# Beginning layer 2's first block beside the last pieces of layer 1's expert network

## The chip, the cores and the metric

The kernel runs on one core of a Trainium2 chip. The number that counts is the device time of one execution in microseconds (us). A core has a matrix engine (PE, with its weight loads shown apart as PEld), a vector engine (DVE), an activation engine (ACT), a general engine (POOL) and queues that start transfers (SP's among them). Each works through its own list of instructions in order; between engines, semaphores say when data is ready.

## The reference, cut to what matters

Four layers run over x of 16 sequences x 256 tokens x 128 features. Each layer has an attention part and a feed-forward part, each behind a normalization, scaled and shifted by modulations. The change touches the end of layer 1 and the beginning of layer 2:

```python
# layer 1, feed-forward part: an encoder layer with 8 experts, 2 chosen for each token
gates = softmax(xf @ gW + gb); top2_scores, top2_idx = top_k(gates, 2)
h = relu(einsum('nd,edf->enf', xf, W1) + b1); y = einsum('enf,efd->end', h, W2) + b2
out = einsum('ne,end->nd', w, y)          # w: the two scores, zero elsewhere
# ... then a layer norm, and x = x + gb * out

# layer 2, attention part: 16 heads of 8 features, causal, with rotary positions
h = layernorm(x) * (1 + ca) + sa
Q, K, V = h @ qw, h @ kw, h @ vw          # by heads of 8
Q, K = rope(Q, freq), rope(K, freq)
score = Q @ K.T / sqrt(128) - 1e10 * (1 - tril)
x = x + ga * (softmax(score) @ V) @ ow
```

## The kernel before, in words

x stays in on-chip memory, turned: 128 features on the partitions and 4096 tokens along them, in 8 blocks of 512 tokens (two sequences each).

**Layer 1's experts** (`layer1_ffn`, `sparse`). The tokens of each half of the batch are sorted into lists by expert. The lists are worked off in pieces of 256 rows that belong to one expert, 23 pieces for each half, 46 in all. A step n of the loop in `sparse` fetches the rows and the weights of piece n + 2 (SP), transposes piece n on PE (`ps_in`) and copies it with DVE (`l_x`), does the first product of piece n - 1 (`hidden`: `ps_hid`, then ReLU on ACT into `s`) and the second product of piece n - 2 (`ps_out`, copied by ACT to `l_o` and stored to `done`). At the end of each step, `advance` is called three times.

**Side work as generators.** `self.later` is a list of generators; `advance` gives each of them one step, up to its next `yield`. `tail(blk)` is such a generator. It gathers, by eight indirect transfers that POOL issues, the two expert rows of each token of a block out of `done`, weights and adds them on DVE (`list_sums`), transposes the sum, normalizes it and adds it into x on POOL; then `self.tailed` goes up by one. Tails of the first half are begun at n = 24 (`NPIECE + 1`), when the first half's pieces are stored. Inside the pieces each gather takes two steps, and nine empty steps come after the gathers.

**Layer 2's attention** (`layer2_attn`, `attend8`). A unit is one sequence. For each unit there are two passes over the scores. The first finds the row maxima: eight steps, each with a causal mask (`ident16` times `half_below`), products of `km` with `q` in two groups of 32 partitions into a tile of 1024 columns, and one DVE reduction (L1382). The second pass makes the exponentials of transposed scores with the maxima subtracted (`qm`, `ps_exp`, ACT at L1387, then on POOL at L1390 the part above the diagonal is zeroed) and multiplies them with the values. The loop over `cycle` does one step of the first pass and one of the second, the first pass ahead by `lead = per + LEAD` = 10 cycles. So cycles -10 to -3 are eight cycles of the first unit's maxima alone.

Ahead of a block's first unit, `prepare` must have run: it waits until the block's tail is done (`self.tailed`), normalizes the block (`modulated_steps`, two products with a matrix of means), projects it and rotates it (`turned8`: for each of four tiles, two products on PE, two multiplications on DVE at L1724 or L1722, one addition on POOL at L1725). Then `start_unit` makes `km` on POOL (L1258). At the end of each cycle `advance` is called once and the next block's `prepare` gets one step.

**Order.** With `self.strict` set, PE's instructions stay in the order in which the program makes them. Those of DVE, ACT, POOL and SP are placed by a planner of the framework, which may put an independent instruction earlier. Most operations of these engines go through the helper at L230, products through L273 and transposes through L276, so tiles' names tell them apart.

Of the kernel before, what the change touches and what calls it, by code (L numbers as in the profile page):

```python
# [9 lines left out]
F32 = mybir.dt.float32  # L10
# [4 lines left out]
ALU = mybir.AluOpType  # L15
AX = mybir.AxisListType
# [3 lines left out]
P = 128  # L20
B, T = 16, 256
NT = B * T
BLK = 512
# [192 lines left out]
def bc(ap, shape):  # L216
    return ap.to_broadcast(shape)


class _InOrder:  # L220


    def __init__(self, kernel, engine):
        self.kernel, self.engine = kernel, engine

    def __getattr__(self, name):
        f = getattr(self.engine, name)

        def run(*args, **kw):
            ins = f(*args, **kw)  # L230
# [4 lines left out]
        return run  # L235


class _Kernel:
# [931 lines left out]
    def spaces8(self, pool, nt, ctx):  # L1170


        nc = self.nc
# [3 lines left out]
        self.ps_one = self.pool("ps_two", 2, PSUM, ctx=ctx)  # L1177
        self.v8, self.m8 = [], []
# [32 lines left out]
    def attend8(self, nt, group, prepare, finish, scale, causal=False, masks=(None, None)):  # L1211

        nc = self.nc
        half = self.c("half")
        NQ = nt * P
        qmask, kmask = masks
# [8 lines left out]
            then = [((0, 1), 0, j0) for j0 in (0, 2)]  # L1227
        per = len(first)
        units = group * NBLK
        U = self.units8 = []  # L1230
        sides = []
        ready = {}
        held = []
# [12 lines left out]
        def prepared(blk):  # L1246
            return prepare(blk, lambda: cycle >= (blk - 1) * group * per)

        def start_unit(u):
            blk, i = divmod(u, group)  # L1250
            if i == 0:
                run(ready.pop(blk))
                if blk + 1 < NBLK:
                    ready[blk + 1] = prepared(blk + 1)
            d = U[u]
            km = d["km"] = self.att.tile([P, 2, 2, NQ], F32, tag="km", name="km")
            for i in range(2):
                nc.gpsimd.tensor_scalar(km[:, :, i, :], d["k"], half[:, i : i + 1], 0.0, ALU.mult, ALU.add)  # L1258

# [72 lines left out]
        self.strict = True  # L1332
        lead = per + self.LEAD
        cycle = -lead
        ready[0] = prepared(0)
        for cycle in range(-lead, units * per):
            mx, ex = cycle + lead, cycle
            mu, mt = divmod(mx, per)
            eu, et = divmod(ex, per)
# [53 lines left out]
            held = []  # L1393
# [25 lines left out]
    def layer1_ffn(self):  # L1419
# [19 lines left out]

        W = self.w.tile([P, 3 * 8 * P], F32, tag="wqkv", name="list_w")[:, : 5 * (4 * P + 2)].rearrange("p (n c) -> p n c", n=5)  # L1440
        with ExitStack() as ctx:
            one = self.pool("f1_one", 1, ctx=ctx)
            gb = one.tile([P, 8], F32, tag="gb", name="gb")
            nc.gpsimd.dma_start(out=gb, in_=self.t["f1_gb"].to_broadcast([P, 8]))

# [28 lines left out]
            with ExitStack() as c2:  # L1474
# [68 lines left out]
            self.sparse("f1_W", [W[:, i] for i in range(5)], [got[:, i] for i in range(4)], hidden, 2 * P, two, ps_in, tail)  # L1543

    def sparse(self, name, W, got, hidden, second, two, ps_in, tail):


        nc = self.nc
# [37 lines left out]
        for n in range(-2, N + 2):  # L1586
            if n + 2 < N:
                fetch(n + 2)
            if 0 <= n < N:
                turn(n)  # L1590
            if 0 <= n - 1 < N:
                hidden(U[n - 1])
            if n >= 2:
                out(n - 2)
            if n == NPIECE + 1:
                self.halves_done = 1
                self.later.append(tail(0))
            for _ in range(3):
                self.advance()
        self.settle()  # L1600
# [64 lines left out]

    def layer2_attn(self):
        nc = self.nc
        w16 = self.load("a2_w", self.w, tag="small", dtype=F16)  # L1670
        w = self.w.tile([P, 10 * P], F32, tag="wo", name="a2_w32")
        nc.vector.tensor_copy(w, w16)
        self.tables()
        with ExitStack() as ctx:
            two = self.pool("a2_two", 2, ctx=ctx)
            one = self.pool("a2_one", 1, ctx=ctx)
            self.ln = self.att = two
            self.spaces8(one, 2, ctx)
            below = self.half_copy(one, "below")

            def prepare(blk, free):
                while self.tailed <= blk:
                    self.advance()
                hb = two.tile([P, BLK], F32, tag="hb", name="hb", bufs=3)
                yield from self.modulated_steps(blk, 2, 0, lambda b: hb[:, (b % 2) * T : (b % 2 + 1) * T])
                while not free():
                    yield
                qk = []
                yield from self.turned8(w, hb, qk)
                at = two.tile([P, BLK], F32, tag="at", name="at", bufs=3)  # L1690
                for i in range(2):
                    self.unit8(qk, hb, at, slice(i * T, (i + 1) * T), w[:, 8 * P : 9 * P], None)
# [10 lines left out]
            self.attend8(2, 2, prepare, finish, 1.0 / 11.3125, True, (below, None))  # L1703
        self.lists_on = False

    def turned8(self, w, hb, out):


        nc = self.nc
        for a in range(2):  # L1710
            o = self.att.tile([P, 2, BLK], F32, tag=f"q8_{a}", name=f"q8_{a}")
            out.append(o)
            for c in range(2):
                t = self.att.tile([P, BLK], F32, tag="rot_t", name="rot_t")
# [476 lines left out]
```

## Time and profile before

| what | value |
|---|---|
| median of three runs | 3257.55 us (3256.97 to 3267.07) |
| the profiled execution: its own time | 3261.82 us |
| its span, first to last instruction | 3260.1 us |
| PE busy | 2858.9 us, 88% of the span |
| DVE busy | 1939.4 us, 59% |
| ACT busy | 1706.1 us, 52% |
| POOL busy | 1395.4 us, 43% |
| last store of a piece begins (ACT's queue) | 2295.80 us |
| first exponential of layer 2 begins (ACT, E from ps_exp) | 2341.58 us |

A row of the timeline reads: start in us, length in us, engine, line of the program, operation, the tile written and the tiles read, shape, number of instructions merged, and in brackets how long the engine had been idle and what ended that. "remote" in brackets means that the release could not be tied to an engine of this core or a known queue. In the table of stretches each engine has busy time and, in brackets, its number of instructions; then come PE's granted clock as a share of full speed, the busy share of the transfer engines, and GB/s.

### The profile page before, as it was taken

Reading aid. Unit: us, or ns where it says so; the run is one execution under the profiler, and the core shown is the slowest. Engines: PE = TensorE matmul, PEld = TensorE weight load, DVE = VectorE, ACT = ScalarE, POOL = GpSimd, SP = SyncE. Lnnn points to the kernel's source line nnn. Section 1 sums busy time; section 2 is a strip of 40 time slices with the busy share of each in tenths; the row PEclk is TensorE's granted clock in tenths of the full one; section 3 lists DMA queues with packets and bytes.
Section 4 is the critical chain, followed back from the end, with each engine's and each line's share of the span. In section 5 each row is a group of like instructions: output and inputs, shape, how many; then the busy total and the mean of one; then the engine's idle time right before and its main releaser. Section 6 shows DMA issues by size and latency. Waiting matters only on the chain. (4 is left out here: it accounts for less than half of the span.)

```text
span 3260.1 us, 51286 instructions
## 1 busy us (share of the span) xinstructions
PE 2858.9 (88%) x18502; PEld 1727.6 (53%) x18502; DVE 1939.4 (59%) x4602; ACT 1706.1 (52%) x4484; POOL 1395.4 (43%) x1254
## 2 busy tenths in 40 slices
PE   5999999897968899999978888876789998999777
PEld 3566665565956677777633333365344444555433
DVE  4777777874435666666645566422566674645564
ACT  3777677574435566666625454433234434665533
POOL 4776777674134533443320022224443332233455
PEclk9999999999989999999989999878999999999998
DMA  8040000001742000000000000155100000000000
GB/s 300 8 46 1 9 6 7 24 7 56 216 138 74 14 3 1 1 1 1 1 1 1 1 14 13 34 160 149 34 9 20 1 1 1 1 1 1 4 10 14
DMA packets 66862, 112.73 MB, mean 35 GB/s; under 512 B 10144, under 2 KB 38880, under 8 KB 66352
## 3 DMA queue, kind: packets, MB, share of 16 engines
q1 hardware_dynamic: 44848, 79.67, 8.9%
q0 software_dynamic: 8512, 17.71, 1.9%
q10 hardware_dynamic: 13248, 12.06, 1.1%
q8 instruction: 147, 2.41, 0.3%
q14 instruction: 107, 0.88, 0.1%
HBM read 70.05 MB, written 43.54 MB: 35 GB/s over the span
## 5 line engine op out<-in xcount | busy, mean ns | idle before, releaser
L230 POOL TENSOR_TENSOR E<-E,sm_inv 128x1024 f32<-128x1024 f32 (+1 forms) x256 | 430.3, 1681 | 438.2 <-PE ps_big L273 172.8
L1387 ACT ACTIVATE E<-ps_exp 128x1024 f32<-128x1024 f32 (+1 forms) x256 | 234.4, 916 | 348.1 <-PE ps_exp L273 266.9
L1382 DVE TENSOR_REDUCE m<-ps_max 128x4 f32<-128x1024 f32 (+1 forms) x246 | 268.6, 1092 | 212.9 <-PE ps_exp L273 149.6
L230 ACT ACTIVATE E<-E,sm_neg 128x256 f32<-128x256 f32 x512 | 254.1, 497 | 212.7 <-DVE sm_neg L1104 208.9
L273 PE MATMUL ps_max<-km,q 32*128 32x512 f32 (+1 forms) x984 | 264.8, 615 | 61.1 <-DVE m L1382 51.4
L276 PEld LDWEIGHTS ps_one<-w_cst,E 128*128 128x128 f32 x1792 | 205.1, 142 | 176.5 <-POOL E L230 116.6
L276 PE MATMUL ps_one<-w_cst,E 128*128 128x128 f32 x1792 | 246.0, 277 | 55.1 <-POOL E L230 49.6
L273 PE MATMUL ps_exp<-qm,q 32*128 32x512 f32 (+1 forms) x1024 | 278.4, 621 | 6.1 <-ACT E L1387 4.5
L230 DVE COPY PT<-ps_one 128x512 f32<-128x512 f32 x320 | 208.9, 685 | 102.3 <-PE ps_one L276 96.7
L273 PE MATMUL ps_big<-kT,qT 64*128 64x256 f32 (+1 forms) x2048 | 268.2, 381 | 0.0
L273 PE MATMUL ps_one<-PT,v 128*64 128x256 f32 (+1 forms) x2048 | 225.6, 363 | 3.3 <-DVE PT L230 3.0
L230 ACT ACTIVATE E<-ps_big,sm_neg 128x128 f32<-128x128 f32 (+1 forms) x512 | 208.8, 423 | 28.4 <-DVE sm_inv L230 22.5
L230 POOL DMA_INDIRECT rows<-list_rows,l_i x128 | 126.2, 986 | 222.2 <-DMA rows<-list_rows,l_i 134.0
L230 POOL TENSOR_TENSOR r_r<-r_r,r_t 128x512 f32<-128x512 f32 x128 | 162.8, 1272 | 134.1 <-DVE r_t L230 114.0
L1104 DVE CUSTOM_DVE_ANT_0 E<-ps_big,bias 128x256 f32<-128x256 f32 x512 | 186.8, 421 | 51.5 <-PE ps_big L273 24.3
L230 POOL DMA_INDIRECT list_rows<-done,origin x128 | 123.1, 962 | 184.1 <-issue 70.6
L273 PEld LDWEIGHTS ps_big<-kT,qT 64*128 64x128 f32 x2048 | 168.5, 189 | 59.0 <-issue 50.1
L273 PEld LDWEIGHTS ps_one<-PT,v 128*64 128x64 f32 x2048 | 133.1, 138 | 81.2 <-DVE sm_inv L230 13.9
L1390 POOL TENSOR_SCALAR_AFFINE_SELECT E<-E 128x512 f32<-128x512 f32 x128 | 82.9, 648 | 192.8 <-ACT E L1387 192.7
L230 DVE TENSOR_REDUCE sm_neg<-ps_big 128x4 f32<-128x512 f32 (+1 forms) x128 | 122.2, 955 | 72.5 <-PE ps_big L273 70.8
L273 PEld LDWEIGHTS ps_max<-km,q 32*128 32x128 f32 x984 | 76.9, 190 | 164.6 <-DVE m L1382 80.6
L273 PE MATMUL ps_rope<-w_a_qkv,hb 128*128 128x512 f32 x256 | 137.9, 623 | 23.0 <-ACT r_sq L230 19.6
(339 smaller groups left out, 6246.8 us busy)
## 6 DMA issues: line engine op xcount, KB each, us to landing
rows<-zeros SPq DMA_DIRECT2D x8, 2048.0 KB
list_w<-in_f_W SPq DMA_DIRECT2D x46, 257.0 KB
done<-l_o ACTq DMA_DIRECT2D x92, 128.0 KB
f_W<-in_f_W SPq DMA_DIRECT2D x27, 386.0 KB
f_room<-in_f_W SPq DMA_DIRECT2D x19, 386.0 KB
list_sums<-rows SPq DMA_DIRECT2D x46, 128.0 KB
rb_rows<-rb_d SPq DMA_DIRECT2D x1, 4088.0 KB
w_a_qkv<-in_a_qkv SPq DMA_DIRECT2D x2, 1536.0 KB
```

The costliest lines, as they stand in the source:

```text
L230: ins = f(*args, **kw)
L273: self.ordered(self.nc.tensor.matmul(out, lhsT, rhs, start=start, stop=stop, **kw))
L276: self.ordered(self.nc.tensor.transpose(out, in_, self.c("ident")))
L1104: nc.vector.tensor_tensor_reduce(e[:, i], S[:, i], bias[g][:, i, off : off + T], 1.0, BIG, ALU.add, ALU.min, neg[:, i : i + 1])
L1382: nc.vector.tensor_reduce(o, Sm[:, :, :, :, :nk], AX.X, ALU.max, negate=True)
L1387: nc.scalar.activation(E, Se[:, :, :, :, q0:], AF.Exp, scale=scale)
L1390: nc.gpsimd.affine_select(D, D, [[0, 4], [1, P]], ALU.is_ge, 0.0, base=0, channel_multiplier=-1)
```

## The change

Layer 2's beginning is cut off as a generator of its own. `attn2_begin`, called in `layer1_ffn` ahead of `sparse`, loads and widens layer 2's attention weights, clears the tiles for values and maxima (`kept8`), and returns `early8`. In `sparse`, at n = 24, this generator goes into `self.later` behind `tail(0)`. It yields until block 0's tail is done, and then does, one step for each advance: `prepare` of block 0 (norm, projections, rotations), `km` of the first unit, and the first unit's maxima in sixteen steps, each with one bank of PSUM, one group of 32 partitions, its own mask and one reduction of half the former size. Then it sets `begun8`.

`attend8` with `begun=True` first runs `advance` until `begun8` is set. Its loop starts at cycle -2 instead of -10: the second unit is started, `prepare` of block 1 is begun, and the first unit's `less_maxima` is put on the list for cycle -2.

The tiles that live across the border (`hb`, `at`, `q8`, `rot_t`, `km`) come from a pool of their own, `begin2`. Room for it is made by putting the small scratch tiles of layer 1's gates into the unused end of a room that is there already (`_Room`).

```diff
+class _Room:
+    def __init__(self, space, pool):
+        self.space, self.pool, self.at, self.of = space, pool, 0, {}
...
+    def early8(self, prepare, qmask):
+        self.units8 = []
+        for _ in prepare(0, lambda: True):
+            yield True
+        d = self.units8[0]
+        km = d["km"] = self.begin2.tile([P, 2, 2, 2 * P], F32, tag="km", name="km")
+        for i in range(2):
+            self.nc.gpsimd.tensor_scalar(km[:, :, i, :], d["k"], self.c("half")[:, i : i + 1], 0.0, ALU.mult, ALU.add)
+        yield True
+        for t in range(2):
+            nk = (t + 1) * P
+            for c in range(2):
+                for g in (2, 3, 0, 1):
+                    o = self.bank().rearrange("p (i k) -> p i k", i=2)[:, :, :nk]
+                    self.mm(o[:, :, nk - P :], self.ident16, bc(qmask.unsqueeze(1), [P, 2, P]), skip_group_check=True)
+                    r = slice(32 * g, 32 * g + 32)
+                    self.mm(o, d["q"][r, c, t * P : (t + 1) * P], km[r, c, :, :nk], start=False, skip_group_check=True)
+                    a = self.m8[0][:, t, 8:9]
+                    m = bass.AP(tensor=a.tensor, offset=a.offset + 2 * P * c + 32 * g, ap=[list(a.ap[0]), [P + 16, 2]])
+                    self.nc.vector.tensor_reduce(m, o, AX.X, ALU.max, negate=True)
+                    yield True
+        self.begun8 = True
...
-        U = self.units8 = []
+        if begun:
+            while not self.begun8:
+                self.advance()
+        else:
+            self.units8 = []
+        U = self.units8
...
-        ready[0] = prepared(0)
-        for cycle in range(-lead, units * per):
+        ready[0] = iter(()) if begun else prepared(0)
+        if begun:
+            start_unit(1)
+            ready[1] = prepared(1)
+            held.append(lambda: less_maxima(0))
+        for cycle in range(-lead + (per if begun else 0), units * per):
...
-            one = self.pool("f1_one", 1, ctx=ctx)
+            one = _Room(self.room_left, self.sm)
...
+            early = self.attn2_begin()
...
                 self.halves_done = 1
                 self.later.append(tail(0))
+                if early:
+                    self.later.append(early)
...
-    def layer2_attn(self):
+    def attn2_begin(self):
         nc = self.nc
         w16 = self.load("a2_w", self.w, tag="small", dtype=F16)
-        w = self.w.tile([P, 10 * P], F32, tag="wo", name="a2_w32")
+        w = self.w2 = self.w.tile([P, 10 * P], F32, tag="wo", name="a2_w32")
         nc.vector.tensor_copy(w, w16)
         self.tables()
+        self.a2 = ExitStack()
+        pool = self.begin2 = self.pool("a2_begin", 2, ctx=self.a2)
+        one = self.pool("a2_one", 1, ctx=self.a2)
+        self.kept8(one, 2)
+        self.below2 = self.half_copy(one, "below")
+        self.begun8 = False
...
+            while self.tailed <= blk:
+                if blk:
+                    self.advance()
+                else:
+                    yield
...
+        self.prepare2 = prepare
+        return self.early8(prepare, self.below2)
```

More of the change, by code (lines that the diff above doesn't have):

```diff
@@ L235, in __getattr__, with tile @@
         return run
+class _Room:
+    def __init__(self, space, pool):
+        self.space, self.pool, self.at, self.of = space, pool, 0, {}
+    def tile(self, shape, dtype, tag, name, bufs=None):
+        if dtype != F32:
+            return self.pool.tile(shape, dtype, tag=tag, name=name)
+        n = int(np.prod(shape[1:]))
+        if tag not in self.of:
+            self.of[tag] = self.at
+            self.at += n
+        v = self.space[:, self.of[tag] : self.of[tag] + n]
+        return v if len(shape) == 2 else v.rearrange("p (a b) -> p a b", b=shape[2])
 class _Kernel:
@@ L1170, in spaces8, with banks8 @@
     def spaces8(self, pool, nt, ctx):
-        nc = self.nc
+        self.banks8(ctx)
+        self.kept8(pool, nt)
+    def banks8(self, ctx):
         self.ps_max = self.pool("ps_max", 1, PSUM, ctx=ctx)
@@ L1177, in spaces8, with kept8 @@
         self.ps_one = self.pool("ps_two", 2, PSUM, ctx=ctx)
+    def kept8(self, pool, nt):
+        nc = self.nc
         self.v8, self.m8 = [], []
@@ L1209, in unit8, with attend8 @@
         self.units8.append(dict(q=q, k=k, hb=hb[:, tok], wv=wv, dst=at[:, tok], bias=bias, whole=(hb, at)))
-    def attend8(self, nt, group, prepare, finish, scale, causal=False, masks=(None, None)):
+    def early8(self, prepare, qmask):
[20 more added lines that the diff above has]
+        self.begun8 = True
+    def attend8(self, nt, group, prepare, finish, scale, causal=False, masks=(None, None), begun=False):
         nc = self.nc
@@ L1255, in start_unit @@
             d = U[u]
-            km = d["km"] = self.att.tile([P, 2, 2, NQ], F32, tag="km", name="km")
+            km = d["km"] = (self.begin2 if begun else self.att).tile([P, 2, 2, NQ], F32, tag="km", name="km")
             for i in range(2):
@@ L1541, in hidden, with sparse @@
                     nc.scalar.activation(s[:, c], pc[c], AF.Relu, bias=d["w"][:, 4 * P + c : 4 * P + c + 1])
-            self.sparse("f1_W", [W[:, i] for i in range(5)], [got[:, i] for i in range(4)], hidden, 2 * P, two, ps_in, tail)
-    def sparse(self, name, W, got, hidden, second, two, ps_in, tail):
+            self.sparse("f1_W", [W[:, i] for i in range(5)], [got[:, i] for i in range(4)], hidden, 2 * P, two, ps_in, tail, early)
+    def sparse(self, name, W, got, hidden, second, two, ps_in, tail, early=None):
         nc = self.nc
@@ L1664, in settle, with prepare @@
             self.advance(True)
-    def layer2_attn(self):
+    def attn2_begin(self):
         nc = self.nc
         w16 = self.load("a2_w", self.w, tag="small", dtype=F16)
-        w = self.w.tile([P, 10 * P], F32, tag="wo", name="a2_w32")
+        w = self.w2 = self.w.tile([P, 10 * P], F32, tag="wo", name="a2_w32")
         nc.vector.tensor_copy(w, w16)
         self.tables()
+        self.a2 = ExitStack()
[4 more added lines that the diff above has]
+        self.begun8 = False
+        def prepare(blk, free):
+            while self.tailed <= blk:
[3 more added lines that the diff above has]
+                    yield
+            hb = pool.tile([P, BLK], F32, tag="hb", name="hb", bufs=3)
+            yield from self.modulated_steps(blk, 2, 0, lambda b: hb[:, (b % 2) * T : (b % 2 + 1) * T])
+            while not free():
+                yield
+            qk = []
+            yield from self.turned8(w, hb, qk)
+            at = pool.tile([P, BLK], F32, tag="at", name="at", bufs=3)
+            for i in range(2):
+                self.unit8(qk, hb, at, slice(i * T, (i + 1) * T), w[:, 8 * P : 9 * P], None)
+        self.prepare2 = prepare
+        return self.early8(prepare, self.below2)
@@ L1674, in layer2_attn @@
+    def layer2_attn(self):
+        nc, w = self.nc, self.w2
         with ExitStack() as ctx:
             two = self.pool("a2_two", 2, ctx=ctx)
-            one = self.pool("a2_one", 1, ctx=ctx)
             self.ln = self.att = two
[L1678 to L1692, printed above, removed]
+            self.banks8(ctx)
@@ L1701, in finish @@
                 yield
-            self.attend8(2, 2, prepare, finish, 1.0 / 11.3125, True, (below, None))
+            self.attend8(2, 2, self.prepare2, finish, 1.0 / 11.3125, True, (self.below2, None), begun=True)
+        self.a2.close()
         self.lists_on = False
@@ L1710, in turned8 @@
         for a in range(2):
-            o = self.att.tile([P, 2, BLK], F32, tag=f"q8_{a}", name=f"q8_{a}")
+            o = self.begin2.tile([P, 2, BLK], F32, tag=f"q8_{a}", name=f"q8_{a}")
             out.append(o)
             for c in range(2):
-                t = self.att.tile([P, BLK], F32, tag="rot_t", name="rot_t")
+                t = self.begin2.tile([P, BLK], F32, tag="rot_t", name="rot_t")
                 for s in range(2):
```

## The prediction

> **What bounds the kernel now.** I read the page first (PE busy 88% of the span, so an idle PE is what can be won), then the chain of work that ended last, which around 2300 us runs through PE, DVE, ACT and POOL in turn. Then I put the table of stretches over the seam between layer 1's pieces and layer 2.
>
> ```profile
> 2257.80:2294.80 37.00, 30.82 (x187) 25.50 (x185) 12.88 (x35) 16.70 (x39) 10.33 (x10) 0.91 0.47 128
> 2294.80:2333.80 39.00, 28.59 (x91) 10.93 (x90) 20.87 (x36) 6.69 (x11) 23.25 (x24) 0.82 0.11 29
> 2333.80:2341.60 7.80, 5.69 (x35) 2.90 (x34) 4.88 (x8) 1.97 (x4) 1.47 (x2) 1.00 0.08 23
> 2341.60:2404.50 62.90, 51.00 (x370) 23.62 (x374) 34.86 (x61) 20.45 (x33) 35.62 (x42) 0.92 0.07 17
> 2518.10:2568.00 49.90, 46.49 (x370) 21.23 (x370) 32.00 (x53) 20.47 (x33) 17.92 (x24) 1.00 0.00 1
> ```
>
> Columns: length, then busy time and instructions of PE, PEld, DVE, ACT, POOL, then granted clock. Row one is the last pieces of layer 1, row two the stretch that the change empties: norm, projections and eight maxima alone. It is 39 us, but PE is busy for 28.6 of them, partly at a lower clock (0.82). So at most 39.0 - 28.6 = 10.4 us of PE idleness and a few us of slow clock can be won there. Row four is the first sixteen cycles, row five a block of sixteen without tails.
>
> The timeline gives the pieces of that stretch:
>
> ```profile
> 2256.78 1.05 PE L273 MATMUL ps_out<-list_w,s 128*128 128x128 f32 x8
> 2258.82 1.27 POOL L230 TENSOR_TENSOR x<-x,ln_xc 128x512 f32<-128x512 f32 x1 [9.89 <-DVE ln_xc L230]
> 2267.76 1.02 PE L273 MATMUL ps_one<-list_sums,w_cst 128*128 128x512 f32 x2
> 2272.56 0.69 DVE L230 TENSOR_TENSOR ln_xc<-list_sums,ps_one 128x512 f32<-128x512 f32 x1 [4.63 <-remote]
> 2273.97 2.08 PE L273 MATMUL ps_one<-ln_sq,w_cst 128*128 128x512 f32 x2 [5.19 <-ACT ln_sq L230]
> 2279.35 1.03 PE L273 MATMUL ps_hid<-l_x,list_w 128*128 128x256 f32 x4
> 2281.32 1.03 PE L273 MATMUL ps_hid<-l_x,list_w 128*128 128x256 f32 x4
> ...
> 2299.78 2.07 PE L273 MATMUL ps_one<-ln_sq,w_cst 128*128 128x512 f32 x2 [3.75 <-ACT ln_sq L230]
> 2304.95 9.76 PE L273 MATMUL ps_one<-hb,a_w 128*128 128x512 f32 x16 [3.10 <-DVE hb L230]
> 2318.43 0.70 PE L273 MATMUL ps_max<-km,q 32*128 32x256 f32 x4 [3.49 <-POOL km L1258]
> 2327.13 1.13 PE L273 MATMUL ps_max<-km,q 32*128 32x512 f32 x4
> 2333.81 0.39 PE L273 MATMUL ps_max<-half_below,ident 128*128 128x256 bf16 x2
> ...
> 2353.91 0.96 POOL L230 DMA_INDIRECT list_rows<-done,origin  x1 [0.28 <-DVE list_sums L230]
> 2362.48 1.23 DVE L1382 TENSOR_REDUCE m<-ps_max 128x4 f32<-128x1024 f32 x1 [4.32 <-remote]
> 2363.76 0.52 PE L273 MATMUL ps_max<-half_below,ident 128*128 128x256 bf16 x2 [3.51 <-DVE m L1382]
> ```
>
> To see: undisturbed pieces follow each other every 1.97 us (2279.35 to 2281.32), and ps_in, ps_hid and ps_out fill 0.38 + 1.03 + 1.05 us of that. The pieces are PE-bound, so work put beside them is paid for, except where PE stands still (2268.8 to 2274.0). Cycle -2, where the changed loop starts, begins at 2333.81.
>
> **When the early steps run.** Tail and early steps get three advances a piece, 72 from n = 24 on. `tail(0)` needs 16 for its gathers, 9 empty ones and 13 more, so it ends at advance 38 (n = 36); the trace agrees, its POOL add is at 2258.82. The early generator follows at once: norm at 38 to 42, projections 43 to 46, km at 47, sixteen maxima at 48 to 63. It ends eight advances before the pieces do.
>
> **What it adds to the pieces (PE).**
> - First mean: PE is free at 2257.8, x is ready at 2260.1: a wait of 2.4. It stands ahead of all later pieces in PE's order.
> - Two means at 1.02: 2.1. Eight projections at 1.04: 8.3.
> - Waits within these: hb comes 0.7 late; two PSUM banks are shared with `tail(1)`, whose bank is held until its four DVE sums (1.12 us) are done: 2.3. Together 3.0.
> - km: DVE 0.75, POOL add 1.26, two km at 0.68, less 0.6 of tail work on PE between: 3.0.
> - Maxima: before, a cycle did two 32-row groups at once: 0.70 us at 256 columns, 1.13 at 512, with two masks at 0.19. Now each group stands alone behind its own full-width mask. A single is put at 0.52 and 1.02 (half of a 1.02 us mean, and all of it). 8 x (0.19 + 0.52) + 8 x (0.19 + 1.02) = 15.4, against 4 x 1.08 + 4 x 1.51 = 10.4 before.
>
> Sum 34.2. The Trainium skill (TensorE: Matmul & The Clock Gate, Why this matters for your kernels) says of a 32-row matmul that it takes the time of a 128-row one and that the gain lies in tiles running at once. That speaks against the change. By the rule's near-free second tile the unpaired steps would cost 6.1 more instead of my 5.0; I keep the row's pair times.
>
> Taken back: the standstill of 5.2 at 2268.8, about 2.5 of slow matmuls behind it (2.08 where 1.02 is usual), and 1.0 at 2284. It falls in a run of eight POOL gathers, and all such runs beside pieces here end in a "remote" wait, so it may only move: between 0 and 8.7, I take 4.5. The pieces then end 29.7 later. DVE's sixteen reductions (a 512-column one 0.69, a 256-column one estimated at 0.39) and ACT's three operations lie beside PE; DVE is busy 12.9 of 37 there. If DVE's order were bad, each late l_x would stop PE; 5 at most.
>
> **What the seam becomes.** Cycle -2 starts about 0.5 after the last piece: 2294.8 + 29.7 + 0.5 = 2325.0, against 2333.8. That is -8.8.
>
> **What the seam no longer hides.** `tail(3)`'s matmuls (0.6 + 1.15 + 0.66 + 1.02) and block 1's norm (2 x 1.02) were in it: 5.5. They now fall into the PE-bound cycles; 1.5 fills the wait for qm: +4.0. Block 1's norm starts eight cycles later, so its last projection is made in a burst at the unit change, and the next km is waited for: 0.75 + 1.26 + 1.36, less PE's masks: +3.0.
> Two runs of gathers, at 2298 and 2325, cost nothing in the seam. They move into the first cycles, queued on POOL ahead of affine_select and km. The two runs that lie there now (from 2353.9 and 2392.9) each stop DVE and PE for about 4 and slow PE's clock after; row four is 13 longer than row five. So 2 x (0 to 6); I take half, +6.
>
> **Moved, no cost.** The weight's load already goes out at 2120.24 (SP), its cast is at 2123.77, the memsets at 2129 to 2139: the planner has them there today, so SP and POOL queues keep their order. Cover: the list building. Without it the cast (0.82) and the twelve memsets (some 4.8 on POOL) would show. The room in place of the small pool only renames scratch space; a false wait there could cost 0 to 2. The table load (1.28, at 2296.16) lies beside PE.
>
> **Sum.** -8.8 + 4.0 + 3.0 + 6.0 = +4.2 us against the profiled run (span 3260.1, its time 3261.82, 1.7 outside the span). That run is 4.3 above the median of 3257.55; on the median it makes 3262.
>
> **Rivals.**
> - *Stalls come back in full (slower).* One mechanism: runs of gathers meeting a busy PE. If the standstill in the pieces stays (+4.5) and both moved runs stop the cycles (+6), and gathers put ahead of km on POOL (eight at 1.25) hold PE before the first maximum by half their length (+5), it is 4.2 + 15.5, about +20: 3277. It decides from two stops of 4 us on. For it: every run beside pieces shows a "remote" wait. Against: the two runs at 2298 and 2325 show none.
> - *The seam is really won (faster).* PE work fills the standstill (-4.2), the moved gathers don't stop (-6), waits in the pieces are halved (-4), km is hidden (-3): -13, so 3245. For it: PE idles 10.4 in the seam and 6.2 in the last pieces. Against: the extra 5.0 of PE work, and PE's order is fixed.
> - *It does not do what it says:* the steps don't finish in the pieces and are run off in one go afterwards. By the count there are eight advances to spare; then the time would stay within 5 of now.
>
> A second rule of the same page (same section: no PE gaps above about 3 us) bears on the 2.4 and 3.0 us waits: by it, a longer one would halve the clock for some 3.4 us, 1.7 more each. The row says as much: 2.07 at 2299.78 after 3.75 idle. I count none, and keep 3 for the range.
>
> **How the numbers follow.** Anything within 0.3% (9.8 us) can't be told from no change. An about even trade has 0.44, of which 0.09 lies above the bound; stalls in full 0.32; the seam won 0.24, of which 0.03 is within. So faster 0.21, same 0.38, slower 0.41. The likeliest case says 3262, its own range 3252 to 3274; the range over the cases, 3246 to 3282.
>
> **What would show it.** Cycle -2's mask within 1 us of the last piece, near 2325; E's first exponential near 2333 instead of 2341.6; pieces ending near 2324; single maxima at 0.5 and 1.0; PE waits of 2 to 3 us before the first mean and the first maximum; "remote" waits in the first sixteen cycles, which last 70 to 76 us instead of 62.9. I am wrong if the pieces end before 2315 or after 2332, or if those cycles stay at 63.

## The result, and the profile after

The changed kernel takes 3269.07 us (median of 20 runs, 3258.59 to 3290.03), the kernel before 3258.06 us in the same comparison (20 runs). The ratio is 1.003, 95% interval 1.0017 to 1.0042: slower by 5.5 to 13.7 us, right at the 0.3% that can be told from no change. The forecast was 3262, with a sum of +4.2 us.

The profiled run takes 3265.54 us (span 3263.8, before 3260.1). That pair of spans, 3.7 us apart, hides most of what the change does. The table cuts both traces at the same events: the start of the first gather of `tail(0)`, the start of its addition into x on POOL, the end of the last `l_o` copy of the pieces, and the start of E's exponential of cycles 0, 16, 32, 48 and 64.

| stretch, us | before | after | difference |
|---|---|---|---|
| first gather to x | 52.8 | 50.8 | -2.0 |
| x to last piece | 36.9 | 72.2 | +35.3 |
| last piece to first exponential | 45.8 | 8.9 | -36.9 |
| cycles 0 to 16 | 62.9 | 77.2 | +14.3 |
| cycles 16 to 32 | 56.9 | 60.4 | +3.5 |
| cycles 32 to 48 | 56.7 | 53.6 | -3.1 |
| cycles 48 to 64 | 49.9 | 51.6 | +1.7 |
| cycle 64 to the last exponential of layer 2 | 190.3 | 187.3 | -3.0 |
| after the last exponential of layer 2 | 501.8 | 499.3 | -2.5 |

From x to cycle 64 the change costs 14.8 us in this pair. The stretches before and behind ran 11.1 us shorter in the second profile (3.6 of it ahead of the first gather); the change moves no PE work there, so this is put down to chance, as the runs of one kernel lie up to 31 us apart. A difference of two spans must be cut by stage before it is read.

The table of stretches of the changed kernel (length, then busy time and instructions of PE, PEld, DVE, ACT and POOL, granted clock, transfer share, GB/s), for the pieces after x, the seam, and the first sixteen cycles:

```profile
2252.20:2324.80 72.60, 61.05 (x259) 37.82 (x258) 28.94 (x63) 18.36 (x43) 17.90 (x18) 0.88 0.24 66
2324.80:2334.40 9.60, 6.70 (x37) 3.40 (x37) 4.74 (x9) 1.91 (x4) 5.74 (x6) 0.82 0.14 42
2334.40:2411.70 77.30, 59.64 (x374) 26.72 (x377) 37.33 (x63) 21.94 (x35) 37.68 (x45) 0.82 0.07 18
```

To see: the seam is now 9.6 us, but in the first sixteen cycles PE is busy for 59.6 us of 77.3 at a clock of 0.82, where before it was 51.0 of 62.9 at 0.92. The instructions are nearly as many (374 against 370): they are slower, and there is more standing still.

The timeline of the changed kernel, the rows that answer to those of the prediction:

```profile
2253.26 1.26 POOL L230 TENSOR_TENSOR x<-x,ln_xc 128x512 f32<-128x512 f32 x1 [8.07 <-DVE ln_xc L230]
2254.57 1.85 PE L290 MATMUL ps_one<-x,w_cst 128*128 128x512 f32 x2 [2.31 <-POOL x L230]
2277.15 0.27 PE L290 MATMUL ps_one<-half_below,ident 128*128 128x256 bf16 x1 [2.01 <-DVE rot_t L1799]
2282.71 1.22 PE L290 MATMUL ps_one<-km,q 32*128 32x256 f32 x2 [5.29 <-POOL km L1243]
...
2295.01 0.69 PE L290 MATMUL ps_one<-km,q 32*128 32x256 f32 x2
2314.04 1.12 PE L290 MATMUL ps_one<-km,q 32*128 32x512 f32 x2
2324.46 0.38 PE L290 MATMUL ps_max<-half_below,ident 128*128 128x256 bf16 x2
2329.39 1.57 PE L290 MATMUL ps_one<-x,w_cst 128*128 128x512 f32 x2 [2.90 <-DVE qm L1324]
2343.53 0.59 PE L290 MATMUL ps_max<-half_below,ident 128*128 128x256 bf16 x2 [4.53 <-DVE m L1440]
...
2371.20 0.80 PE L290 MATMUL ps_max<-km,q 32*128 32x256 f32 x2 [3.49 <-POOL km L1312]
```

To see: the wait of 2.31 us before the first mean is there, and one of 5.29 before the first maximum's product. A product of one group alone takes 0.69 us at 256 columns and 1.12 at 512. Cycle -2 (`ps_max`, 2324.46) follows the pieces at once. The cycles stand still ahead of 2343.53, where PE waits for a maximum of DVE, and ahead of 2371.20, where it waits for km.

DVE's and POOL's timelines of the changed kernel around the first of these standstills (rows left out):

```profile
2342.79 0.69 DVE L1440 TENSOR_REDUCE m<-ps_max 128x4 f32<-128x512 f32 x1 [3.22 <-remote]
```

```profile
2328.70 1.00 POOL L230 DMA_INDIRECT list_rows<-done,origin  x1
...
2338.50 0.65 POOL L1448 TENSOR_SCALAR_AFFINE_SELECT E<-E 128x512 f32<-128x512 f32 x1
...
2346.97 0.95 POOL L230 DMA_INDIRECT list_rows<-done,origin  x1 [0.30 <-issue]
2347.93 0.64 POOL L1448 TENSOR_SCALAR_AFFINE_SELECT E<-E 128x512 f32<-128x512 f32 x1
```

DVE's maximum had stood 3.22 us behind a "remote" wait, as the runs of gathers in the kernel before show it too; a second one, of 4.79, comes at 2349.90. And from 2328.70 to 2347.93 fifteen gathers, one each 1.26 us, follow each other on POOL with a single affine_select between them. The second affine_select, which the products with the values need, comes 9.4 us after the first.

### The profile page after: what moved, and what is told of

It reads as the page before. It is cut to its first block, busy times and chain, and to the rows that moved or that the text cites. A ratio compares the mean times of both kernels' runs of the same rounds, so it can differ in the third digit from the quotient of the medians.

```text
span 3263.8 us, 51269 instructions
## 1 busy us (share of the span) xinstructions
PE 2872.6 (88%) x18502; PEld 1735.5 (53%) x18502; DVE 1937.1 (59%) x4610; ACT 1704.7 (52%) x4484; POOL 1394.5 (43%) x1254
## 5 line engine op out<-in xcount | busy, mean ns | idle before, releaser
L293 PE MATMUL ps_one<-w_cst,E 128*128 128x128 f32 x1792 | 247.1, 278 | 55.4 <-POOL E L230 49.1
```

Source lines behind the costliest of these rows:

```text
L293: self.ordered(self.nc.tensor.transpose(out, in_, self.c("ident")))
```

## The experiments

They ran on three other chips (e1 to e4, e5 to e8, e9 to e12), on which the kernel before takes 3194 to 3198 us, so each is given as its ratio to the kernel before on its own chip. "Pieces" is the stretch from x to the last piece, "seam" from there to the first exponential; these times come from one profiled run each, and are often compared across chips. The tables of stretches below are cut up to 0.5 us beside the table's events. Only e10 and e12 came out about as expected. e1 cannot be told from no effect, e9 lies between its theories, and for the others the expected size was missed, mostly on the small side.

| kernel | ratio | 95% interval | pieces | seam | 0-16 | 16-32 | 32-48 | 48-64 |
|---|---|---|---|---|---|---|---|---|
| before (e6) | 1 | | 29.7 | 44.2 | 57.5 | 63.0 | 59.8 | 49.9 |
| changed (e5) | 1.0099 | 1.0076 to 1.0121 | 79.9 | 10.2 | 75.4 | 60.7 | 56.8 | 51.6 |
| changed, groups two at a time (e1) | 1.0076 | 1.0054 to 1.0099 | 74.3 | 10.2 | 75.1 | 60.5 | 56.8 | 52.6 |
| changed, early steps after the pieces (e4) | 1.0074 | 1.0052 to 1.0095 | 28.5 | 67.0 | 68.7 | 58.9 | 52.0 | 53.0 |
| before, groups one at a time (e7) | 1.0079 | 1.0058 to 1.0100 | 28.5 | 72.1 | 58.7 | 62.3 | 56.7 | 49.9 |
| changed, empty steps (e11) | 1.0021 | 1.0010 to 1.0032 | 63.6 | 8.0 | 73.8 | 60.5 | 54.3 | 51.6 |
| changed, gathers held (e2) | 1.0005 | 0.9993 to 1.0016 | 68.1 | 8.9 | 62.9 | 55.4 | 54.5 | 54.6 |
| before, gathers held (e9) | 0.9959 | 0.9946 to 0.9971 | 31.0 | 44.8 | 55.1 | 55.3 | 56.9 | 49.9 |
| maxima left in the loop (e3) | 0.9976 | 0.9965 to 0.9988 | 48.1 | 19.6 | 58.4 | 62.5 | 56.7 | 49.9 |
| the same, gathers held (e8) | 0.9915 | 0.9892 to 0.9937 | 44.6 | 19.6 | 52.7 | 55.3 | 59.9 | 49.9 |
| the same again (e10) | 0.9930 | 0.9914 to 0.9946 | 44.6 | 19.6 | 52.7 | 55.3 | 60.0 | 49.9 |
| changed, all three mended (e12) | 0.9987 | 0.9978 to 0.9997 | 64.3 | 8.9 | 62.7 | 55.4 | 54.6 | 51.6 |

**The two kernels again (e5, e6).** No edit.

> The changed kernel itself again, as a yardstick for the other runs on this chip (before takes some 3195 us where e1 to e4 ran, 2% less than in the first comparison). Theory A and B: the same ratio as in the first comparison, 1.002 to 1.005. If a chip whose transfers are quicker leaves PE fewer stops to fill, the ratio is higher, up to 1.008, as for e1 and e4; e1 would then be no slower than the control, and pairing worth nothing.

> The kernel before again, for its trace on this chip: POOL's addition to x of tail 0 to the end of the pieces 37 us, from there to the first exponential 45 us, the first sixteen cycles 63 us, as in the first trace, give or take 4.

Tables of stretches, of the kernel before (pieces after x, seam, first sixteen cycles) and then of the changed one (pieces, first sixteen cycles):

```profile
2196.00:2226.10 30.10, 27.52 (x172) 22.40 (x170) 12.18 (x32) 15.96 (x37) 10.78 (x11) 1.00 0.54 155
2226.10:2269.90 43.80, 32.96 (x121) 13.36 (x121) 24.92 (x43) 7.70 (x11) 24.76 (x25) 0.84 0.10 28
2269.90:2327.40 57.50, 49.27 (x362) 22.87 (x362) 35.16 (x61) 20.51 (x32) 31.45 (x37) 0.94 0.06 15
```

```profile
2200.90:2280.90 80.00, 69.55 (x262) 42.23 (x263) 28.48 (x61) 18.79 (x42) 17.89 (x18) 0.79 0.20 57
2291.10:2366.50 75.40, 61.64 (x366) 26.91 (x368) 36.70 (x63) 21.97 (x35) 36.97 (x44) 0.79 0.07 17
```

PE's two longest waits of the changed kernel in these sixteen cycles (sum, times, longest):

```profile
PE ps_out L290 <- POOL E L1448: 7.7, 3, 4.0
PE ps_max L290 <- POOL km L1312: 3.5, 1, 3.5
```

Here the last pieces of the kernel before stand at full clock, PE busy 27.5 of 30.1, without the standstill that the first chip shows. There is next to nothing to fill, and the change costs 1.0% instead of 0.3%. PE's own work grows from 27.5 to 69.6 us, its clock falls from 1.00 to 0.79. In the first sixteen cycles DVE shows no "remote" wait on this chip; PE stands still for POOL. The wait for km is not new (3.7 us in e6), the 7.7 for the affine_selects are. By these rows the sixteen cycles grow by 12.4 us of PE's busy time, at a clock of 0.79 instead of 0.94, and by 5.5 of standing still.

**The maxima's pairing (e1, e4, e7).** In e1 the changed kernel's early maxima go two groups at a time:

```diff
-                for g in (2, 3, 0, 1):
-                    o = self.bank()...
-                    self.mm(o[:, :, nk - P :], self.ident16, ...)
-                    self.mm(o, d["q"][r, c, ...], km[r, c, :, :nk], start=False, ...)
+                for j0 in (2, 0):
+                    os = [self.bank()... for _ in range(2)]
+                    for o in os:
+                        self.mm(o[:, :, nk - P :], self.ident16, ...)
+                    for g, o in enumerate(os, j0):
+                        self.mm(o, d["q"][r, c, ...], km[r, c, :, :nk], start=False, ...)
...
```

> Changed kernel, but the early maxima come in eight steps of two row groups each: both masks first, then the two products side by side, each in its own bank. Theory A (the early work costs what it takes on a PE-bound stage: lost pairing 5 us, waits at its start about 10 with slow clock, runs of POOL gathers and km in the first cycles about 14): 5 us less than the changed kernel, some 3264 against 3269; two products at 512 columns take about 1.13 us together instead of 2 x 1.12. Theory B (the price is in the runs of gathers alone): no difference over 2 us. Theory C (the scratch room and pools kept over the border cost it, not the moved steps): no difference.

In e4 all early steps, single groups as they are, are run off behind the pieces, with an `advance` between some of them:

```diff
-                if early:
-                    self.later.append(early)
+                self.early = early
...
-            while not self.begun8:
-                self.advance()
+            self.strict = True
+            for i, _ in enumerate(self.early):
+                if i > 10 and i % 2:
+                    self.advance()
```

> Changed kernel, but the early steps are not run beside the pieces: they are run off after the last piece, with one advance of the tails for every second maximum (eight in all, as before). All else of the change stays: scratch room, pools over the border, loop entered at cycle -2, block 1's norm begun there, maxima in single groups. Theory A: the seam is as in before plus the unpaired maxima (5) and block 1's norm and km (up to 5): 3260 to 3268, and the pieces end as in before. Theory B: as before, 3258 to 3262. Theory C: as slow as the changed kernel or slower, 3269 and more.

In e7 nothing of the change is in. The kernel before gets, in its ten lead cycles alone, another order on PE: mask, product, mask, product, instead of both masks and then both products. Instructions and shapes are the same.

```diff
-                if qmask is not None:
+                if qmask is not None and live_e:
...
-            for c, o, lhsT, rhs, fresh in sorted(mms, ...):
+            for j, (c, o, lhsT, rhs, fresh) in enumerate(sorted(mms, ...)):
+                if qmask is not None and not live_e:
+                    z = Sm[:, j, :, :, nk - P : nk]...
+                    self.mm(z, self.ident16, ...)
                 self.mm(o, ...)
```

> The kernel before, and only PE's order in the ten lead cycles of layer 2 is changed: each group of 32 rows gets its mask right ahead of its product, so that two products never stand side by side (no other instruction is added, moved or left out). Theory A as the prediction had it (lost pairing is 5 us of product time): 3 to 6 us slower. Theory D, from e4's trace (1.22 and 2.07 us a single product, where a single took 0.69 and 1.12 in the changed kernel: PE's granted clock stays at half while it has only single groups): 8 to 16 us slower, and products of the lead cycles at 1.2 and 2.0 us. If pairing is covered by the waits for DVE there: no difference.

e7's table of stretches, for the seam:

```profile
2233.50:2305.30 71.80, 61.48 (x121) 22.82 (x122) 25.74 (x43) 7.74 (x12) 24.59 (x25) 0.59 0.06 17
```

Its timeline:

```profile
2255.73 0.69 PE L273 MATMUL ps_max<-km,q 32*128 32x256 f32 x2 [3.60 <-POOL km L1258]
2269.20 1.22 PE L273 MATMUL ps_exp<-km,q 32*128 32x256 f32 x2
2280.06 2.07 PE L273 MATMUL ps_exp<-km,q 32*128 32x512 f32 x2
```

And the timeline of the kernel before on the same chip (x4: two groups):

```profile
2248.32 0.70 PE L273 MATMUL ps_max<-km,q 32*128 32x256 f32 x4 [3.49 <-POOL km L1258]
2251.10 1.22 PE L273 MATMUL ps_exp<-km,q 32*128 32x256 f32 x4
2256.08 0.70 PE L273 MATMUL ps_exp<-km,q 32*128 32x256 f32 x4
2258.90 1.13 PE L273 MATMUL ps_exp<-km,q 32*128 32x512 f32 x4
```

Two readings. First, two groups side by side take 0.70 us and one alone 0.69: the second is free. Second, both kernels make their first product after the same km wait at full speed, and both then fall to half: the paired one has 1.22 us at 2251.10. But the paired one is back at full speed after some 3.4 us, and the unpaired one stays at 1.22 and 2.07 us a product to the end of the seam, though PE is busy back to back: its granted clock is 0.50 from 2256.9 to 2305.3, with PE busy for 48.3 of these 48.4 us. PE's busy time grows from 33.0 to 61.5 us for the same 121 instructions, and the seam by 28. e4 shows the same in the changed kernel's own steps when no pieces lie between them: 67.0 us of seam, single products at 1.22 and 2.07. e7 takes the pairs apart and also makes PE change between mask and product at every step; which of the two keeps the clock down, it does not separate.

e1, two groups at a time inside the pieces, shortens them from 79.9 to 74.3 us: PE's busy time falls by 10.2, its standing still grows by 4.6, as steps now wait for DVE. The ratio goes from 1.0099 to 1.0076, and the intervals overlap.

**The waits at the start (e11).** The changed kernel with empty steps ahead of block 0's norm and ahead of the maxima, so that x and km are ready when PE comes to them:

```diff
         # after km
-        yield True
+        for _ in range(4):
+            yield True
...
         # before hb, the norm's result
+            if blk == 0:
+                yield
+                yield
+                yield
```

> The changed kernel with three empty steps between the normalised rows and block 0's norm, and three more after km, so that TensorE waits for neither; all else as in the change. Theory (the two waits of 2.3 and 5.3 us cost their own length and leave TensorE's clock at half for a while after): stretch from x to the last piece 80 us in the control, 70 to 74 here, ratio 1.0099 down to 1.007. Rival (the half clock comes from the single products alone, and the waits cost only their length, some of which moves elsewhere): 73 to 77 us and 1.008 to 1.009.

The pieces take 63.6 us instead of 79.9, a larger gain than I had expected, and the ratio goes from 1.0099 to 1.0021. The table of stretches of e11 for the pieces and the first sixteen cycles:

```profile
2193.20:2256.50 63.30, 58.55 (x242) 35.35 (x242) 28.70 (x62) 17.65 (x39) 18.02 (x18) 0.92 0.25 70
...
2264.80:2338.60 73.80, 54.61 (x374) 24.54 (x377) 37.11 (x63) 21.69 (x35) 38.15 (x45) 0.88 0.07 20
```

Its timeline, single groups between pieces:

```profile
2225.04 0.28 PE L290 MATMUL ps_one<-half_below,ident 128*128 128x256 bf16 x1
2225.25 0.69 PE L290 MATMUL ps_one<-km,q 32*128 32x256 f32 x2
2225.88 0.28 PE L290 MATMUL ps_one<-half_below,ident 128*128 128x256 bf16 x1
...
2232.14 0.69 PE L290 MATMUL ps_one<-km,q 32*128 32x256 f32 x2
2233.24 1.92 PE L290 MATMUL ps_hid<-l_x,list_w 128*128 128x256 f32 x4
...
2237.28 0.28 PE L290 MATMUL ps_one<-half_below,ident 128*128 128x256 bf16 x1
2237.49 1.12 PE L290 MATMUL ps_one<-km,q 32*128 32x512 f32 x2
2238.55 0.28 PE L290 MATMUL ps_one<-half_below,ident 128*128 128x256 bf16 x1
```

And a row of the changed kernel's timeline (e5), just behind its km wait:

```profile
2230.36 1.22 PE L290 MATMUL ps_one<-km,q 32*128 32x256 f32 x2 [5.29 <-POOL km L1243]
```

With the km wait gone the singles run at 0.69 and 1.12 us (one took 1.24); with it they begin at half speed. But they are not free of the clock even so. Twice it falls to 0.50 for some 3.4 us, at 2232.8 and at 2239.7, each time right behind three single steps, and the first products of the piece that follows take 1.92 and 1.91 us instead of 1.03. PE had not stood still for over 14 us before the first of these falls, nor between them. So the loss of clock is not the waits' alone.

The difference of 16.7 us between the two rows (80.00 and 63.30) has three parts. PE stands still for 10.5 us in e5 and 4.8 in e11: 5.7 less. The 242 instructions are 20 fewer than e5's 262, because in e11 PE does one more piece ahead of x instead of waiting for it: some 2.0, the distance of two undisturbed pieces. The other 9.0, an estimate by subtraction, is PE's busy time at a better clock (0.79 to 0.92). How long half speed lasts behind a wait is not fixed: behind the same 5.29 us for km the clock stays at 0.50 for 16.5 us in e5, and for 6.2 in the first trace of the changed kernel.

**The gathers (e2, e9).** The planner may put the tails' gathers early on POOL. Here those of layer 1's experts are kept in program order there, in e2 on the changed kernel and in e9 on the kernel before:

```diff
+        self.pinned = name == "f1_W"
...
-                self.gps.indirect_dma_start(g[:, t, i], None, self.done[half][:, :], of)
+                ins = self.gps.indirect_dma_start(g[:, t, i], None, self.done[half][:, :], of)
+                if self.pinned:
+                    self.tc.keep_in_program_order(ins)
```

> Changed kernel, but the gathers of layer 1's tails keep the program's order on POOL (each behind the POOL instruction made before it), so the planner can't put a run of eight ahead of the rotations' additions, km or affine_select. Theory A: the wait for the first km falls from 5.3 to about 3 us, the first sixteen cycles from 77 to 66-70 us, together 8 to 12 us less than the changed kernel: 3257 to 3261. Theory B: the same or more, 10 to 14 less. Theory C: no difference. If the stops come from the transfers' number and not from their coming in runs, there is no gain either.

> The kernel before, with only the tails' 16 gathers of the hidden products kept in program order on GpSimd's queue. Theory (what the run with three moves and the held gathers gained, 0.9915, is a sum: 0.9976 from the moved norm, projections, rotations and km, and the rest from the held gathers): the held gathers alone give about 0.994 here, some 18 us (the first sixteen cycles of the kernel before then shorter than 57.5 us, the next sixteen shorter than 63.0). Rival (the held gathers pay only where the change has put other work of GpSimd late, as in the changed kernel): 0.998 to 1.001. Second rival (all of the 0.9915 is the held gathers, and the move is worth nothing): 0.991 to 0.992.

The table of stretches of e2, first sixteen cycles:

```profile
2277.40:2340.30 62.90, 54.23 (x374) 24.34 (x376) 36.68 (x63) 21.93 (x35) 31.01 (x37) 0.89 0.04 13
```

POOL's timeline of e2 in these cycles:

```profile
2278.92 0.95 POOL L230 DMA_INDIRECT list_rows<-done,origin  x1 [0.15 <-issue]
2281.31 0.94 POOL L1448 TENSOR_SCALAR_AFFINE_SELECT E<-E 128x512 f32<-128x512 f32 x1 [1.44 <-ACT E L1445]
2282.41 0.95 POOL L230 DMA_INDIRECT list_rows<-done,origin  x1 [0.15 <-issue]
```

Gathers and affine_selects alternate, and sixteen cycles take 62.9 us instead of 75.4. The pieces gain as well (79.9 to 68.1): fewer gathers lie between the rotations' additions on which km waits, and PE's wait for km falls from 5.29 to 2.53 us. Together the ratio goes from 1.0099 to 1.0005. The kernel before gains too, 0.9959, with all 64 gathers of layer 1's tails held (the text before the run says 16); the waits of its PE in cycles 16 to 32 held 4.3 us for affine_select in e6, and hold none when the gathers are kept. So the order on POOL is a cost that both kernels pay, and the changed one pays more.

**Only norm, projections, rotations and km moved (e3, e8, e10).** The early generator ends behind km; the loop starts at cycle -10 as before:

```diff
-        yield True
+        self.begun8 = True
+        return
...
-        for cycle in range(-lead + (per if begun else 0), units * per):
+        for cycle in range(-lead, units * per):
...
-            if mx == 0:
+            if mx == 0 and not begun:
```

e8 and e10 are one kernel: this, the held gathers and the three empty steps before the norm.

> Changed kernel with one part undone: norm, projections, rotations and km of block 0 stay beside the pieces, the first unit's maxima go back into the loop (cycles -10 to -3, in pairs), which again hold block 1's norm, tail 3 and a run of gathers. Theory A: pieces end 13 to 16 us earlier than in the changed kernel, eight cycles of about 2 us come back, and the first sixteen cycles fall from 77 to about 65; together 8 to 14 less than the changed kernel, 3255 to 3261, level with before or slightly under. Theory B: near the same, 8 to 12 less. Theory C: no difference, 3269.

> e3 (maxima stay in the loop) with e2 (gathers pinned to the program's order on POOL) and three spare steps ahead of block 0's norm, so that a piece stands on PE before the first mean. Theory A: what e2 and e3 save adds up in part, since both take gathers off the first cycles: 4 to 10 us under e3's 0.9976, a ratio of 0.994 to 0.997. If e3 already has all of it: 0.9976 again. Theory B: as A.

> The version with norm, projections, rotations and km moved, the maxima left in the loop and the gathers held, once more, on the same chip as the kernel before with the gathers held. Theory: 0.991 to 0.993 again, and 5 to 10 us below the kernel before with the gathers held; rival (the move is worth nothing once the gathers are held): the two within 3 us.

The table of stretches of e8: pieces, seam, first sixteen cycles.

```profile
2202.00:2246.70 44.70, 39.91 (x208) 28.67 (x207) 19.45 (x45) 18.80 (x42) 22.74 (x23) 0.96 0.41 111
2246.70:2266.30 19.60, 18.75 (x97) 8.59 (x97) 17.07 (x31) 4.55 (x8) 9.02 (x9) 1.00 0.13 35
2266.30:2319.00 52.70, 46.72 (x368) 22.01 (x371) 35.92 (x61) 20.49 (x33) 31.14 (x38) 1.00 0.06 15
```

Here PE is busy 18.75 of the seam's 19.6 us, all of it at full clock, where e6 had it standing still for 10.8 of 43.8. Without the held gathers the move alone gives 0.9976. On one chip, the held gathers alone (e9) take 3184.70 us and all three together (e10) 3173.79: the move with its empty steps is worth 10.9 us even then. This version beats both kernels. It keeps the change's scratch room and its tiles across the border, so these are not what costs time (theory C).

**All three mended (e12).** The full change with e1's, e2's and e11's edits together.

> The full change with its three costs mended at once: maxima two groups at a time, empty steps before norm and maxima, the gathers held. Theory (these three are what the change loses; the clock follows the products that lie side by side): stretch from x to the last piece 60 to 66 us, first sixteen cycles about 60, ratio 0.996 to 1.000, that is, still behind the version that leaves the maxima in the loop. Rival (moving the maxima is good in itself and only the three costs hide it): 0.990 or below.

```profile
2193.30:2257.30 64.00, 55.42 (x255) 34.94 (x253) 27.27 (x60) 18.48 (x42) 22.80 (x23) 0.87 0.28 78
2266.60:2329.30 62.70, 54.02 (x374) 24.15 (x376) 36.64 (x63) 21.88 (x35) 31.00 (x37) 0.89 0.04 13
```

These rows of e12's table of stretches are pieces and first sixteen cycles. It comes to 0.9987, 19 us behind e10 on the same chip. By stage, against e10: pieces and seam together 73.2 instead of 64.3 us, the first sixteen cycles 62.7 instead of 52.7, in which PE waits 3.5 us for km again. Pairing adds nothing to the pieces here: 64.3 us against e11's 63.6. Several steps in them now wait for DVE, 0.5 to 0.9 us each, likely because one step asks for two banks at once. What pairing is worth without that wait wasn't tried.

## Why the prediction was nearly right, and where it failed

In sum: forecast +4.2 us, measured 11.0 between the medians (by the interval 5.5 to 13.7). The mechanism held: work put beside PE-bound pieces is paid for, the gathers become dear in the cycles. The sizes were too small, and both parts on the same side: from x to the first exponential -1.6 came out instead of -8.8, from there to cycle 64 +16.4 instead of +13.0.

- **Pieces +29.7: measured +35.3.** The gross sum of 34.2 is best read on e5's chip, where there is nothing to take back: there the pieces grow by 50.2 us (29.7 to 79.9). Standing still was about right, 8.4 in the sum and 7.9 by the rows of e5 and e6. PE's work was put at 25.8 and grew by 42.0, some 2.0 of it a piece that moved behind x. What failed is the step "I count none" for the clock after the waits: it fell from 1.00 to 0.79. And km was put at 3.0; the wait is 5.29, behind another of 2.01 for a rotation, since gathers lie between the rotations' additions on POOL (with them held, in e2, it is 2.53). The Trainium skill (TensorE: Matmul & The Clock Gate, Why this matters for your kernels) warns of gaps above about 3 us; the prediction weighed it and took too little. By its estimate from the page's rule a long wait costs 1.7 us of slow clock; half speed behind the km wait lasted 6.2 us in the first trace and 16.5 in e5, which loses 3.1 and 8.3. And half speed also came behind single steps without a wait (e11), which the prediction did not consider.
- **Singles at 0.5 and 1.0: measured 0.69 and 1.12**, the time of a pair. The row was read wrongly: half of a full-width product's time was no bound for a 32-row one. The same section's rule, that the gain of 32-row tiles is that they run at once, gave 6.1 for the lost pairing; e11's distances (0.84 and 1.27 from one step to the next, 8 x 0.84 + 8 x 1.27 = 16.9 instead of 15.4) give 6.5 over the 10.4 before. The rule was right and my 5.0 too small. Rows were also read as if they stood end to end: a piece's 0.38 + 1.03 + 1.05 = 2.46 us overlap and fit into 1.97, so sums of row lengths come out somewhat high. That hid a little of the other errors.
- **Taken back 4.5: likely all of 7 to 8.** No "remote" wait of PE, DVE or ACT is left in the changed trace's pieces. The stretch of the kernel before is 36.9 us on the first chip and 29.7 in e6, so 7.2 was there to win. That it is the same 7.2 is argued from the two chips, not shown by a run. It is about half of why the change costs less on the first chip: from x to cycle 64 it costs 14.8 us there and 30.5 in e5 against e6. The other half lies in the changed kernel's own pieces, 72.2 and 79.9 us at clocks of 0.88 and 0.79. Why the clock came back sooner on the first chip stays open.
- **Cycle -2 at 2325, first exponential at 2333: 2324.46 and 2334.44.** The signs were met, but partly by chance. The changed run reached x 5.6 us earlier (2253.26 for 2258.82). From x to the first exponential it gains 1.6 us (82.8 to 81.2), where -8.8 was forecast. A sign given as an absolute time needs a common start.
- **Norms no longer hidden 4.0, km 3.0: held in sum.** With the gathers held in both kernels, the first sixteen cycles differ by 62.9 - 55.1 = 7.8 us, against 7.0. PE waits 3.5 us for km in e2 and not at all in e9. But the 4.0 is right partly by luck: of PE's 4.7 us more of busy time, about 3.5, estimated from the clocks (0.89 in e2, 0.94 in e9), are slow clock and not the norm's work.
- **Gathers in the first cycles +6.0: too small.** On the later chips the cycles grow by 17.9 us, and by 7.8 with the gathers held: 10.1 for the gathers. This lies in the stated 0 to 12, near its upper end. The mechanism was half seen. The forecast "remote" waits are there on the first chip (3.22 and 4.79 us on DVE). On the chip of e5 there are none, and the runs cost as much: there it is the affine_selects, queued behind them on POOL, for which PE waits 7.7 us, and the slow clock around these waits. How the two share the loss on the first chip stays open, as the gathers were not held there.
- **First sixteen cycles 70 to 76: 77.2.** The nearest rival "stalls in full" (+20) put gathers ahead of km at +5, and in the pieces of the changed kernel they do lie between the rotations' additions and km. The profile's own difference, 14.8 from x to cycle 64, lies between the two cases.

## What to carry to other kernels

Before work moves from an idle stretch into one that an engine bounds, its price must be read there: e3 and e8 gain, because norm, projections and km no longer leave PE standing still in the seam; the maxima, which PE pays for in full, lose. Every wait that the moved work brings counts with the clock behind it, and a step or two of slack ahead of a consumer is cheap. And where a planner orders a queue by itself, look at what stands behind a run of gathers: on one chip, holding them in place was worth 13.7 us to the kernel before (3198.41 to 3184.70), more than the 10.9 of the best move.

## What the runs showed of the hardware

Products of one 32-row group at a time, each behind its mask and with no pieces between them, leave PE's granted clock at half although PE never stands still: 0.50 over the last 48.4 us of e7's seam, PE busy for 48.3 of them. The order in pairs, after the same wait, is back at full speed after some 3.4 us. Among full-width pieces the same singles mostly run at full speed (e11), but the clock still falls for 3.4 us at a time behind runs of them, with no wait ahead. So being busy is not all that the clock follows here; whether it follows the rows in use, the changes between mask and product, or something else is open.

Chips differ in places, not by a factor. Of the 70.2 us between the spans of the kernel before on the first chip and in e6 (3260.1 and 3189.9), 40.1 lie ahead of the first gather, 22.7 between it and x, and 7.2 in the last pieces; the rest, over 900 us, is the same in sum to within 1 us. What the "remote" waits of the first chip wait for, no trace here shows.
